# Pairwise bilinear products: x tiles and output slots in one SBUF tile, slots of 43 to 127 pairs

## The chip, the cores and the metric

The kernel runs on one core of a Trainium2 chip. The metric is the device time of one execution in microseconds (us); four runs of a kernel give its median. Beside them stands one profiled execution, whose trace records every instruction and every DMA packet. PE is the matrix engine, DVE the vector engine, SP the engine that here only issues DMAs.

## What is computed

For each of 4096 samples there are 32 fields of 64 numbers. Every field is multiplied by one 64 x 64 matrix, and for each of the 496 pairs of fields i < j the untransformed field i is multiplied, number by number, with the transformed field j:

```python
r_x:       (4096, 32, 64) float32
L0_rec_W:  (64, 64) float32

vid = jnp.einsum('bfd,de->bfe', x, W)
idx_i, idx_j = jnp.triu_indices(32, k=1)
return x[:, idx_i, :] * vid[:, idx_j, :]        # (4096, 496, 64)
```

Input is 33.6 MB, output 520.1 MB.

## The kernel before

The batch is cut into 16 tiles of 256 samples. In a tile, the 128 SBUF partitions are 2 halves of 64 features, and along a partition lie 32 fields of 128 samples (C = 128); a field of a partition is thus 512 bytes, an x tile 16 KiB of each partition, 2 MB in all. The host lays x out that way, pads each row of x in DRAM by 8 fields and each row of the output by 24, and puts the output back in order afterwards.

For a tile t, PE multiplies x by W into `vid`, which takes all of PSUM (L127: 8 groups of 4 fields, 2 halves each). DVE then multiplies pairs: one `tensor_tensor` (L151) takes a run of pairs, with x from SBUF and `vid` from PSUM as operands, and writes 128 x (pairs x 128) numbers to an output slot in SBUF. The order of the pairs is that of `by_block`, a recursive order in which runs are long; `products` cuts the runs where a slot ends, so the slot's size decides how many multiplies there are: 384 here.

Pairs are numbered through all 16 tiles, 0 to 7935, and slots know nothing of tiles. A slot has 84 pairs, 43,008 bytes of a partition (L135 to L155). Three slots are used in turn (`opool`, bufs=3). When a slot is full, SP stores it to its columns of the output with one DMA of 128 rows: 94 stores of 84 pairs, and one of 40 at the end.

x has 6 places (`xpool`). At the start SP loads tile 0 in four pieces and tiles 1 to 5 whole (L113). After the products of tile 4 it loads tiles 6 to 10, and after those of tile 9 tiles 11 to 15.

SP issues in the order in which the program is written. A DMA that must wait, for DVE to fill a slot or for a place of x to be used up, holds back all that is written after it. DVE, too, runs in program order; it writes to a slot only once the slot's earlier store has landed. The framework derives these waits from the places that each instruction reads and writes. Completions are counted on eight semaphores used in turn, so a DMA also waits for the one eight before it.

Of the kernel before, what the change touches and what calls it, by code (L numbers as in the profile page):

```python
# [1 line left out]

# [4 lines left out]

F32 = mybir.dt.float32
ALU = mybir.AluOpType

P = 128

C = 128

SLOT = 84

PLACES = 6

XPAD = 8
OPAD = 24  # L20


def by_block():


    def within(lo):
        yield "step", lo, 2, 1, 0
        for k in range(2):
            yield "step", lo, 4, 2, k
        for i in (lo, lo + 8):  # L30
            yield "row", i + 4, i, 4, 4
        yield "row", lo + 8, lo, 8, 8

    yield from within(0)
    yield "row", 16, 0, 16, 16
    yield from within(16)


def products(blocks, at=0):

    for kind, a, b, c, d in blocks:
        if kind == "row":
            rows, n, i0, di, j0, dj = c, d, b, 0, a, 1
        else:
            rows, n, i0, di, j0, dj = 16 // b, c, a, b, a + c + d, b
        r = k = 0
        while r < rows:
            room = SLOT - at % SLOT
            if k or room < n:
                m, w = 1, min(n - k, room)  # L50
            else:
                m, w = min(rows - r, room // n), n
            yield at, m, w, i0 + r * di + k, di, j0 + r * dj, dj
            at += m * w
            if k + w == n:
                r, k = r + m, 0
            else:
                k += w


def pairs(blocks):

    for _, m, w, i, di, j, dj in products(blocks):
        for r in range(m):
            for k in range(w):
                yield i + r * di + k, j + r * dj


@with_exitstack
def pairwise_bilinear_kernel(  # L70
    ctx: ExitStack,
    tc: tile.TileContext,
    x: bass.AP,
    w: bass.AP,
    out: bass.AP,
):

    nc = tc.nc
    NT = x.shape[0]
    F = x.shape[2] - XPAD
    D = P // 2
    NP = F * (F - 1) // 2

    BANK = 512 // C


    ctx.enter_context(tc.manual_schedule(engines={mybir.EngineType.SP}))  # L90

    const = ctx.enter_context(tc.tile_pool(name="const", bufs=1))
    xpool = ctx.enter_context(tc.tile_pool(name="x", bufs=PLACES))
    opool = ctx.enter_context(tc.tile_pool(name="out", bufs=3))
    psum = ctx.enter_context(
        tc.tile_pool(name="ps", bufs=1, space=bass.MemoryType.PSUM)
    )
    vid = psum.tile([P, F, C], F32)


    w2 = const.tile([P, D], F32)
    nc.sync.dma_start(out=w2, in_=w)  # L102

    loaded = []

    def load(pieces=1):
        t = len(loaded)
        if t == NT:
            return
        xt = xpool.tile([P, F, C], F32, tag="x", name=f"x_{t}")  # L110
        n = F // pieces
        for lo in range(0, F, n):
            nc.sync.dma_start(out=xt[:, lo : lo + n, :], in_=x[t][:, lo : lo + n, :])  # L113
        loaded.append(xt)

    load(4)
    for _ in range(PLACES - 1):
        load()

    for t in range(NT):  # L120
        xt = loaded[t]


        for b in range(0, F, BANK):
            for h in range(2):
                half = slice(h * D, (h + 1) * D)
                nc.tensor.matmul(  # L127
                    vid[half, b : b + BANK, :],
                    lhsT=w2[half, :],
                    rhs=xt[half, b : b + BANK, :],  # L130
                    start=True,
                    stop=True,
                )

        for at, m, w, i, di, j, dj in products(by_block(), t * NP):  # L135
            base = at - at % SLOT
            if at == base:
                ot = opool.tile([P, SLOT, C], F32, tag="o", name=f"o_{at}")
            n = m * w
            o = ot[:, at - base : at - base + n, :]  # L140
            if m == 1:
                left = xt[:, i : i + w, :]
                right = vid[:, j : j + 1, :].to_broadcast([P, w, C])
            else:
                o = o.rearrange("p (m w) c -> p m w c", m=m)
                right = vid[:, j : j + (m - 1) * dj + 1 : dj, :].unsqueeze(2).to_broadcast([P, m, w, C])
                if di == 0:
                    left = xt[:, i : i + w, :].unsqueeze(1).to_broadcast([P, m, w, C])
                else:
                    left = xt.rearrange("p (m d) c -> p m d c", d=di)[:, i // di : i // di + m, i % di : i % di + w, :]  # L150
            nc.vector.tensor_tensor(o, left, right, ALU.mult)  # L151
            at += n
            if at in (base + SLOT, NT * NP):
                nc.sync.dma_start(
                    out=out[:, base:at, :], in_=ot[:, : at - base, :]  # L155
                )


        if (t + 1) % (PLACES - 1) == 0:
            for _ in range(PLACES - 1):  # L160
                load()


_INS = ["r_x", "L0_rec_W"]
_OUTS = [((4096, 496, 64), "float32")]


# [37 lines left out]
```

## Time and profile before

| | us |
|---|---|
| median of 4 runs | 1290.59 (1290.42 to 1290.79) |
| the profiled execution | 1290.72 |
| its span, first to last instruction | 1288.9 |
| DVE busy, 384 multiplies | 1091.3 |
| PE busy, 512 matmuls | 224.2 |
| DVE waiting for stores to land | 160.1 |

The profile's page lists the DMAs by the line that issues them, with their size and the median time from issue to landing:

```profile
out_dram<-o SPq DMA_DIRECT2D x94, 5376.0 KB, 26.5
x<-in_r_x_dram SPq DMA_DIRECT2D x15, 2048.0 KB, 35.0
out_dram<-o SPq DMA_DIRECT2D x1, 2560.0 KB, 25.8
x<-in_r_x_dram SPq DMA_DIRECT2D x4, 512.0 KB, 5.4
```

A store is issued when DVE has filled its slot, and then lies in the queue behind the store before it; so the 26.5 us to landing hold about two transfers of 5.4 MB.

The page shows the bytes that the DMA engines moved, in 40 equal slices of the span:

```profile
GB/s 384 434 446 430 427 441 432 428 438 434 431 431 415 436 430 433 438 430 432 438 432 430 439 430 432 412 438 431 431 439 431 431 439 432 428 438 434 428 436 366
```

The first slice holds the start of the first loads, the 13th and the 26th (415 and 412) the two later groups of loads, the last one the end of the last store.

### The profile page before, as it was taken

The page shows a single profiled execution, that of the slowest core. Times are in us where ns is not written, and L with a number is a line of the kernel's source. Part 1 is how long each engine was busy: PE and PEld are TensorE (multiplying, and loading weights), DVE is VectorE, ACT ScalarE, POOL GpSimd, SP SyncE. Part 2 cuts the span into 40 slices and gives each one's busy share as a digit, 9 for nine tenths or more (in the row PEclk, how much of TensorE's full clock was granted, in tenths as well). Part 3 has the DMA queues.
Part 4 walks back from the last instruction along what each step waited for, and adds up shares of the span by engine and source line. Part 5 has one row for each costly group of instructions (what it writes and reads, how often), then busy time and mean ns, then how long its engine had stood idle before and what let it go on. Part 6 is the DMA issues. An engine that isn't in the chain of part 4 may idle for free.

```text
span 1288.9 us, 1785 instructions
## 1 busy us (share of the span) xinstructions
PE 224.2 (17%) x512; PEld 40.3 (3%) x512; DVE 1091.3 (85%) x384; POOL 0.2 (0%) x4
## 2 busy tenths in 40 slices
PE   4031211303122012030311301103021130312000
PEld 1000000000000000000000000000000000000000
DVE  6998888989897288898989989468989898988881
POOL 0000000000000000000000000000000000000000
PEclk7565565556556555555555655656555555655555
DMA  9999999999999999999999999999999999999998
GB/s 384 434 446 430 427 441 432 428 438 434 431 431 415 436 430 433 438 430 432 438 432 430 439 430 432 412 438 431 431 439 431 431 439 432 428 438 434 428 436 366
DMA packets 16570, 553.80 MB, mean 430 GB/s; under 512 B 1968, under 2 KB 1968, under 8 KB 2480
## 3 DMA queue, kind: packets, MB, share of 16 engines
q1 hardware_dynamic: 16560, 553.69, 99.7%
q8 instruction: 4, 0.07, 0.0%
q14 instruction: 6, 0.05, 0.0%
HBM read 33.59 MB, written 520.09 MB: 430 GB/s over the span
## 4 chain that ended last, share of the span: by engine, by line
DMA 60%; DVE 33%; another core or an unknown queue 5%; issue 0%; PE 0%; DVEq 0%; SPq 0%
DMA out_dram<-o 60%; DVE o L151 33%; PE vid L127 0%; DMA x<-in_r_x_dram 0%; DVEq L151 0%; SPq L102 0%
## 5 line engine op out<-in xcount | busy, mean ns | idle before, releaser
L151 DVE TENSOR_TENSOR o<-x,vid 128x1024 f32<-128x1024 f32 (+9 forms) x384 | 1091.3, 2905 | 170.8 <-DMA out_dram<-o 160.1
L127 PE MATMUL vid<-x,w 64*64 64x512 f32 x512 | 224.2, 995 | 966.3 <-DVE o L151 911.0
L127 PEld LDWEIGHTS vid<-x,w 64*64 64x64 f32 x512 | 40.3, 195 | 1148.6 <-DVE o L151 1060.6
L175 POOL MEMSET const-bfloat16-1.0<- 128x1 bf16 x1 | 0.1, 101 | 0.0
L175 POOL MEMSET const-uint8-127<- 128x1 uint8 x1 | 0.1, 101 | 0.0
L175 POOL MEMSET const-float32-0.0<- 128x1 f32 x1 | 0.1, 98 | 0.2 <-issue 0.2
L175 POOL MEMSET const-float32-1.0<- 128x1 f32 x1 | 0.1, 98 | 0.0
## 6 DMA issues: line engine op xcount, KB each, us to landing
out_dram<-o SPq DMA_DIRECT2D x94, 5376.0 KB, 26.5
x<-in_r_x_dram SPq DMA_DIRECT2D x15, 2048.0 KB, 35.0
out_dram<-o SPq DMA_DIRECT2D x1, 2560.0 KB, 25.8
x<-in_r_x_dram SPq DMA_DIRECT2D x4, 512.0 KB, 5.4
w<-in_L_rec_W_dram SPq DMA_DIRECT2D x1, 32.0 KB, 1.8
```

The lines of the kernel that those rows point to most:

```text
L127: nc.tensor.matmul(vid[half, b : b + BANK, :], lhsT=w2[half, :], rhs=xt[half, b : b + BANK, :], start=True, stop=True,)
L151: nc.vector.tensor_tensor(o, left, right, ALU.mult)
L175: nc = _bacc.Bacc("TRN2", target_bir_lowering=False, num_devices=1, dynamic_dma_scratch_size=1024)
```

## The change

x places and output slots are cut from one SBUF tile, `mem`, of 445 fields (pairs) of each partition, 227,840 bytes; before, the two pools had 6 x 32 + 3 x 84 = 444. `XPLACE` gives the place of each x tile in it, and `SLOTS` a list of 80 slots by size (43 to 127 pairs) and place. `STARTS` has the number of the first pair of each slot. Slots may lie where x tiles have been used up: tiles 0 to 4 and 6 to 10 take places 285 to 444, tile 5 takes 0 to 31, and tiles 11 to 15 take 128, 96, 64, 32 and 0. 58 of the 80 slots have more than 84 pairs, 8 have 84, and 14 fewer.

The loads keep their number, their sizes and their groups (6, 5 and 5 tiles, after the products of tiles 4 and 9). The order of the pairs is unchanged; runs are cut at other places, into 407 multiplies. In the changed file the matmul is at L150, the multiply at L174, the store at L177 and the load at L135.

```diff
-SLOT = 84
-
-PLACES = 6
+UNITS = 445
+
+GROUPS = [6, 5, 5]
+XPLACE = [285, 317, 349, 381, 413, 0, 285, 317, 349, 381, 413, 128, 96, 64, 32, 0]
+SLOTS = [
+    (127, 32), (126, 159), (63, 32), (64, 95), (84, 159), (63, 32),
...
+    (127, 243), (116, 127), (95, 32), (127, 243), (116, 127), (43, 370),
+    (95, 32), (95, 127), (63, 222), (95, 32), (84, 127), (74, 211),
...
+    (105, 0), (106, 105), (56, 211), (95, 267), (51, 362), (107, 160),
...
+    (116, 223), (106, 339), (127, 64), (127, 191), (127, 318), (127, 32),
+    (127, 159), (120, 286),
+]
+STARTS = [0, *accumulate(n for n, _ in SLOTS)]
...
-            room = SLOT - at % SLOT
+            room = STARTS[bisect_right(STARTS, at)] - at
...
-    xpool = ctx.enter_context(tc.tile_pool(name="x", bufs=PLACES))
-    opool = ctx.enter_context(tc.tile_pool(name="out", bufs=3))
+    mem = const.tile([P, UNITS, C], F32)
...
-        xt = xpool.tile([P, F, C], F32, tag="x", name=f"x_{t}")
+        xt = mem[:, XPLACE[t] : XPLACE[t] + F, :]
...
-            base = at - at % SLOT
-            if at == base:
-                ot = opool.tile([P, SLOT, C], F32, tag="o", name=f"o_{at}")
+            slot = bisect_right(STARTS, at) - 1
             n = m * w
-            o = ot[:, at - base : at - base + n, :]
+            begin, end = STARTS[slot], STARTS[slot + 1]
+            ot = mem[:, SLOTS[slot][1] : SLOTS[slot][1] + SLOTS[slot][0], :]
+            o = ot[:, at - begin : at - begin + n, :]
...
-            if at in (base + SLOT, NT * NP):
-                nc.sync.dma_start(
-                    out=out[:, base:at, :], in_=ot[:, : at - base, :]
-                )
+            if at == end:
+                nc.sync.dma_start(out=out[:, begin:end, :], in_=ot)
-        if (t + 1) % (PLACES - 1) == 0:
-            for _ in range(PLACES - 1):
+        if t + 2 == len(loaded) < NT:
+            for _ in range(next(groups)):
                 load()
```

In the prediction, slots, stores and x tiles are numbered from 0.

## The prediction

> **What bounds the kernel now.** I read the page's DMA rows first, since the kernel writes 520 MB, then the chain of waits, the waits of each engine, and the multiplies by shape; last, the trace's DMA packet records, grouped by size. The page:
>
> ```profile
> span 1288.9 us, 1785 instructions
> PE 224.2 (17%) x512; PEld 40.3 (3%) x512; DVE 1091.3 (85%) x384; POOL 0.2 (0%) x4
> DMA  9999999999999999999999999999999999999998
> q1 hardware_dynamic: 16560, 553.69, 99.7%
> HBM read 33.59 MB, written 520.09 MB: 430 GB/s over the span
> ```
>
> The one queue that SP fills keeps the 16 DMA engines occupied for 99.7% of the span; VectorE (DVE) has 15% to spare. The chain of waits, in a steady stretch (start us, length us, what):
>
> ```profile
> 1000.31 26.54 DMA out_dram<-o
> 1026.94 11.56 DVE o L151 x4
> 1038.52 26.50 DMA out_dram<-o
> 1065.11 11.49 DVE o L151 x3
> 1076.62 26.56 DMA out_dram<-o
> 1103.28 11.62 DVE o L151 x5
> 1114.92 26.51 DMA out_dram<-o
> ```
>
> The chain alternates because a slot is written again as soon as its store has landed. From 1000.31 to 1114.92 are nine stores of 84 pairs: 114.61 / 9 = 12.73 us each. A DVE slot takes 11.5 us, so DVE waits for the DMA, never the reverse, as the waits of DVE say:
>
> ```profile
> DVE o L151 <- DMA out_dram<-o: 160.1, 92, 27.1
> ```
>
> (us in total, times, longest.) So only the sum of what the DMA engines must do, and any hole in their work, can move the end.
>
> The packet records price that work. A DMA of 128 rows is 128 packets, 8 to each engine, and a 4-byte completion on each. Commonest durations: 4,096 bytes 159 ns, 16,384 611, 20,480 761, 43,008 1,589, loads and stores alike; a completion 9 ns. The line through the last two is (1589 - 761) / (43008 - 20480) = 0.03675 ns per byte and 8.3 ns for the packet itself; it gives 159 and 611 for the other two sizes. A pair is 512 bytes of a row, so a store of n pairs takes 8 x (8.3 + 18.82 n) + 9 ns = 0.075 + 0.1505 n us: 12.72 for 84, as in the chain. Packets lie end to end from 10 us to 1280 us.
>
> What the packets took above that line adds up to 4.5 us per engine on average: 1.1 at the first loads and the first stores after them, 1.5 around the loads of 390 to 430 us, 1.3 at those of 800 to 830, the rest scattered. The engines do not share it equally: the first is done at 1283.5 us, the average one at 1284.7, the last at 1287.45.
>
> **The change, part by part.**
>
> *Fewer, longer stores.* 95 stores become 80 with the same 7,936 pairs. No bytes go. 15 x 128 packets go, 120 per engine at 8.3 ns: 1.00 us. 15 completions at 9 ns: 0.13 us. Sum: -1.13 us, on the path that sets the end. 58 of the stores have rows longer than 43,008 bytes (up to 127 x 512 = 65,024), which no row here shows. Bounds per such packet: below, its bytes at the rate seen with no fixed part (-8.3 ns); above, the line once more broken in two, +8.3 ns. 58 x 8 = 464 such packets per engine make this -3.9 to +3.9 us. I take 0, as four sizes lie on one line.
>
> The Trainium skill's "DMA: Bandwidth & Descriptors" (Anatomy of one DMA) puts a fixed cost of about 2.0 us on each DMA, of the path that GpSimd issues. By that rule 15 stores fewer would be an estimated 30 us, a time near 1260; the chain's 12.73 us for bytes that take 12.65 at the packet rate leaves 0.08 us per store, so I go by the row.
>
> *Multiplies.* Other slot edges cut the same products into 407 multiplies in place of 384.
>
> ```profile
> L151 DVE TENSOR_TENSOR o<-x,vid 128x8192 f32<-128x8192 f32 x32 | 277.8, 8681 | 1.9 <-DMA out_dram<-o 1.9
> L151 DVE TENSOR_TENSOR o<-x,vid 128x1024 f32<-128x1024 f32 x129 | 151.8, 1216 | 62.3 <-DMA out_dram<-o 51.6 <-PE vid L127 10.6
> ```
>
> (8681 - 1216) / 7168 is 1.041 ns an element, 133.3 ns a pair. 84-pair slots in the chain take 11.43 us with 2 multiplies and 11.75 with 7: 0.064 us for each more. 23 more: 1.5 us of DVE, under the 160.1 us in which it waits for stores. Without that cover it would cost those 1.5 us. 83 more groups of multiplies in the built stream wait on DVE's own earlier ones, since x and slots now share a tile; at most the 0.15 us fixed part of a 1216 ns multiply each, 12 us in all, again inside the 160.
>
> *First store later.* Slot 0 has 127 pairs in 7 multiplies. DVE starts at 10.63 us; 127 x 0.1336 + 7 x 0.064 = 17.4, so the store is issued near 28.1 us and not 22.4. From issue to first packet took 1.0 us at the start (0.73 to 1.73). The loads occupy the engines until 32.6 to 33.7 us, so 29.1 is in time by 3.5 us. Cost 0; if the loads were done sooner, each us would count.
>
> *Slots that wait for others.* Store 0 then ends near 33.0 + 19.2 = 52.2. Slot 1 (126 pairs) is ready at 45.2: in time by 6. Slots 2 and 3 lie where slot 0 was; they start once it has landed (0.45 us after the last packet, as at the end of the trace, and 0.7 for the late engines): 53.4 + 8.6 + 8.8 = 70.8. Slot 4 needs store 1 landed, 71.2 + 1.2 = 72.4, and is ready at 84.0, its first packet 85.0; stores 2 and 3 occupy the DMA until 71.2 + 9.6 + 9.7 = 90.5. In time by 5.5 us. I carried these two columns (ready, and DMA free) on through all 80 stores. After slot 4 the least is 7 us, at store 10 and at the load of x_11; in the later part DVE is up to 20 us ahead.
>
> *Loads.* x_6 to x_10 are issued after store 24, and the last of their places is freed by store 23; store 24 and two loads, 14.4 + 2 x 4.9 = 24 us, lie in the queue meanwhile. x_11 waits for store 49, whose place it takes; SP, which issues in order, stands still, and behind x_11 wait four loads and store 51, whose products are ready. Store 50 alone, 56 pairs, 8.5 us, covers the landing and the issue, 0.45 + 1.0. In time by 7 us; uncovered it would cost 1.5 us. The loads' own bytes and packets are unchanged.
>
> *End.* The last store grows from 40 to 120 pairs, but its slot is ready some 20 us before the DMA gets to it, where before it was 14. The spread between engines stays as it is. Cost 0.
>
> Sum: the profiled execution took 1290.72 us, 1.8 of it around the span; less 1.13 is 1289.6. That run lies 0.13 over the median 1290.59, so the median becomes 1289.5.
>
> **Rivals.**
>
> *Faster than the sum (1287.3).* The 4.5 us above the line and the 2.75 us by which the last engine trails the average belong to no byte. If the extras around the two later load groups fell more evenly, the last engine could gain up to that 2.75. The floor is 1284.5: the changed packets by the line alone, 1279.3 us per engine, 1.9 before the first of them, 1.5 from the last to the end of the span, 1.8 around it. For it: these extras lie where loads meet stores, and the stores beside them change. Against it: there are still three groups of loads, of the same tiles. With half of the two groups' 2.8 us gone and 0.8 of the spread, 2.2 in all: 1289.5 - 2.2 = 1287.3.
>
> *Slower: long rows cost more than the line (1293.4).* Place: packets over 43,008 bytes, at every one of the 58 longer stores. Break-even is 1.13 us / 464 = 2.4 ns a packet. At one more fixed part each, 8.3 ns, it is +3.9: 1289.5 + 3.9 = 1293.4, just over the bound for slower. For it: nothing so long is in the trace. Against it: no bend from 4,096 to 43,008.
>
> *Slower: a hole at x_11 or store 4.* Decides when landing plus issue takes over 8.5 us (now 1.5). To lose the 3.8 us that reach 1293.3 it would have to be 12.3. In the chain DVE starts 0.1 us after a landing (1000.31 + 26.54 = 1026.85; it starts at 1026.94), which speaks against it.
>
> *It doesn't do what it says.* If one tile made every multiply wait for every store, DVE and DMA would take turns, 1091 + 1280 = 2370 us. The built streams' waits name single stores.
>
> **How the numbers follow.** No change is what lies within 0.2%, 2.6 us, about what a measurement of this kernel can tell: 1288.0 to 1293.2. Forecast 0.64 (own range 1288.4 to 1290.7: 0.4 of spread from run to run and 0.8 for extras that fall on other engines), faster 0.20, long rows 0.12, a hole 0.03, false waits 0.01. So faster 0.20, within 0.64, slower 0.16. The range 1287.0 to 1292.2 leaves out the long-row case at its full price, the hole, the false waits and the best quarter of the faster case, 0.2 in all; it takes in some 6 of the 8.3 ns of the long-row bound.
>
> **What would show it.** 14,400 packets on the queue in place of 16,560 (15 x 144 fewer, completions among them); 99.7% occupied again; packets of 65,024 bytes at 2,398 ns (another figure there falls the size term); no slice under 400 GB/s but the first and the last; store 0 issued near 28 us; SP standing before x_11 with DMA full. A DMA slice with a hole, or GB/s that falls where rows are longest, would make the prediction wrong; so would a last engine that trails by more than 2.75 us.

## The result, and the profile after

The changed kernel takes 1289.29 us (median of 41 runs, 1288.93 to 1290.16), the kernel before 1290.61 (61 runs, 1290.19 to 1291.36). The ratio is 0.999, its 95% interval 0.9986 to 0.9995: 1.3 us faster, between 0.6 and 1.8. The forecast was 1289.5. The profiled execution took 1289.63 us, 1.09 less than that of before.

The page of the changed kernel, the rows that answer to those of before:

```profile
span 1287.9 us, 1768 instructions
PE 221.9 (17%) x512; PEld 41.0 (3%) x512; DVE 1087.9 (84%) x407; POOL 0.2 (0%) x4
DMA  9999999999999999999999999999999999999998
GB/s 387 451 416 443 426 430 448 433 435 431 424 435 412 433 435 431 439 428 438 429 444 437 422 438 421 426 431 436 430 437 435 432 433 437 435 433 433 430 442 359
q1 hardware_dynamic: 14400, 553.69, 99.7%
HBM read 33.59 MB, written 520.09 MB: 430 GB/s over the span
```

The bytes are the same and the occupied share is the same, 99.7%; only the packets are fewer, 14,400 for 16,560, as counted in the prediction. No slice but the first and the last is under 412 GB/s, and by the packet records an engine stood idle for some 0.1 us on average between 10 us and the end of the first engine (before: 0.2): the DMA never ran dry.

The packet records of the new sizes, beside what the line drawn through the sizes of before gives (8.3 ns and 0.03675 ns a byte):

| bytes of a packet | by the line, ns | commonest in the trace of the changed kernel, ns |
|---|---|---|
| 22,016 | 817 | 818 |
| 48,640 | 1796 | 1796 |
| 59,392 | 2191 | 2192 |
| 65,024 | 2398 | 2399 |

The first multiplies and gaps of DVE (start us, length us, what, and in brackets the idle time before it and what ended it):

```profile
10.86 34.47 DVE L174 TENSOR_TENSOR mem<-mem,vid 128x1024 f32<-128x1024 f32 x10 [10.86 <-PE vid L150]
53.20 17.41 DVE L174 TENSOR_TENSOR mem<-mem,vid 128x1408 f32<-128x1408 f32 x6 [7.87 <-DMA out_dram<-mem]
72.20 30.66 DVE L174 TENSOR_TENSOR mem<-mem,vid 128x512 f32<-128x512 f32 x17 [1.58 <-issue]
```

Slots 0 and 1 are filled without a break, from 10.86 to 45.3; then DVE stands for 7.87 us until store 0 has landed (the prediction had 53.4 for the 53.20 here, and 72.4 for the 72.20). The DMAs that SP issued:

```profile
28.36 334.62 SPq L177 DMA_DIRECT2D out_dram<-mem  x25
363.16 25.05 SPq L135 DMA_DIRECT2D mem<-in_r_x_dram  x5
392.03 382.87 SPq L177 DMA_DIRECT2D out_dram<-mem  x26
798.75 5.68 SPq L135 DMA_DIRECT2D mem<-in_r_x_dram  x5
804.47 439.43 SPq L177 DMA_DIRECT2D out_dram<-mem  x29
```

The first store goes out at 28.36 (28.1 foretold). Before the loads at 798.75 SP stood still for store 49, the longer of two such waits of SP's queue (us in total, times, longest):

```profile
SPq L135 <- DMA out_dram<-mem: 43.4, 2, 23.8
```

These 23.8 us cost nothing: by the packet records store 50 occupied the engines from 795.4 to 806.7, and the first packet of x_11 began at 804.4, on the engine that was done first. The other wait, 19.6 us, lies inside the load group issued from 363.16 on. And DVE waits less often, but not much less in all, with fewer and longer slots (before: 160.1 us in 92 waits):

```profile
DVE mem L174 <- DMA out_dram<-mem: 143.1, 34, 27.3
```

### The profile page after: what moved, and what is told of

It is laid out like the page before. It is cut to its first block, busy times and chain, and to the rows that moved or that the text cites. A ratio compares the mean times of both kernels' runs of the same rounds, so it can differ in the third digit from the quotient of the medians.

```text
span 1287.9 us, 1768 instructions
## 1 busy us (share of the span) xinstructions
PE 221.9 (17%) x512; PEld 41.0 (3%) x512; DVE 1087.9 (84%) x407; POOL 0.2 (0%) x4
## 3 DMA queue, kind: packets, MB, share of 16 engines
q1 hardware_dynamic: 14400, 553.69, 99.7%
## 4 chain that ended last, share of the span: by engine, by line
DMA 48%; DVE 45%; issue 3%; SPq 0%; PE 0%; another core or an unknown queue 0%; DVEq 0%
DMA out_dram<-mem 47%; DVE mem L174 45%; SPq L135 0%; PE vid L150 0%; DMA mem<-in_r_x_dram 0%; DVEq L214 0%; DVEq L174 0%; SPq L126 0%
## 5 line engine op out<-in xcount | busy, mean ns | idle before, releaser
L174 DVE TENSOR_TENSOR mem<-mem,vid 128x1024 f32<-128x1024 f32 (+16 forms) x407 | 1087.9, 2748 | 155.7 <-DMA out_dram<-mem 143.1
L150 PE MATMUL vid<-mem,w 64*64 64x512 f32 x512 | 221.9, 990 | 953.7 <-DVE mem L174 901.2
L150 PEld LDWEIGHTS vid<-mem,w 64*64 64x64 f32 x512 | 41.0, 196 | 1132.9 <-DVE mem L174 1044.4
```

What stands on the lines that cost most here:

```text
L150: nc.tensor.matmul(vid[half, b : b + BANK, :], lhsT=w2[half, :], rhs=xt[half, b : b + BANK, :], start=True, stop=True,)
```

## The experiments

"Theory" in the expectations is that of the prediction. Each time stands beside runs of the kernel before on the same chip.

### e1: twice the stores

```diff
-                nc.sync.dma_start(
-                    out=out[:, base:at, :], in_=ot[:, : at - base, :]
-                )
+                half = (at - base) // 2
+                for lo in (0, half):
+                    nc.sync.dma_start(
+                        out=out[:, base + lo : base + lo + half, :], in_=ot[:, lo : lo + half, :]
+                    )
```

> The kernel before, with each of its 95 stores issued as two DMAs of half the slot, from the same slot and after the same multiply: 95 stores more, 128 packets and 16 completions each, the same bytes. Theory (8.3 ns a packet, 9 ns a completion, per DMA engine, on the path): 95 x 0.075 = +7.1 us, 1297.7. Rival (a large fixed cost of a DMA, about 2 us each): +190 us, 1480. Rival (packets and completions are hidden, the gain of the change came from elsewhere): 0, 1290.6.

Measured: 1298.32 us beside 1290.78, ratio 1.0058 (1.0045 to 1.0072). That is 7.54 us for 95 more stores, 79 ns each (61 to 98); 75 were expected. A microsecond or two per store is ruled out, and so is nothing. Of the 79 ns, 9 are the completion by its own record, so some 8.8 ns fall on each of the eight packets of an engine.

### e2: twice the packets, the same stores

```diff
+                half = (at - base) // 2
+                place = base + 2 * (base // SLOT)
+                to = out[:, place : place + 2 * (half + 1), :].rearrange("p (h n) c -> p h n c", h=2)
                 nc.sync.dma_start(
-                    out=out[:, base:at, :], in_=ot[:, : at - base, :]
+                    out=to[:, :, :half, :],
+                    in_=ot[:, : at - base, :].rearrange("p (h n) c -> p h n c", h=2),
                 )
...
-    laid = (2 * D, NT * shape[1] + OPAD, C)
+    laid = (2 * D, NT * shape[1] + 488, C)
...
```

(What is left out picks the two parts of each row out of the wider output again, on the host.)

> The kernel before, with each store still one DMA, but its rows in two parts that lie apart in the output: 128 packets more for each of 95 stores, no completion more. Theory: 95 x 8 x 8.3 ns = +6.3 us, 1296.9, and packets of 21,504 bytes take 799 ns. If what costs is the DMA or its completion and not the packet: 0 to +0.9 us, 1290.6 to 1291.5.

Measured: 1299.20 us beside 1290.78, ratio 1.0066 (1.0050 to 1.0081): +8.4 us, 11 ns a packet (8.5 to 13.8). So it is the packet that costs, not the DMA nor its completion. The size is over the 8.3 ns of the line, though its interval meets that of e1. The commonest packet of 21,504 bytes takes the expected 799 ns, but the mean is 803.7, where 43,008 bytes had a mean only 2 ns over their commonest. Rows of the output also lie at another pitch here; but in e1, where the pitch is that of before, packets of this size have a mean of 802.7 too, so the pitch does not explain the longer mean.

### e3: the shared tile alone

```diff
-XPLACE = [285, 317, 349, 381, 413, 0, 285, 317, 349, 381, 413, 128, 96, 64, 32, 0]
+XPLACE = [32 * (t % 6) for t in range(16)]
-SLOTS = [
...
-]
+SLOTS = [(min(84, 7936 - at), 192 + 84 * (at // 84 % 3)) for at in range(0, 7936, 84)]
```

(against the changed kernel)

> The changed kernel with slots of 84 pairs at three places and x at six places of the one tile, as before: 95 stores. Theory (only the number of packets counts): 1290.6. Rival (the shared tile itself changes waits or the speed of DVE or DMA): for the whole of the gain to come from it, 1289.3; if it costs something that the longer slots gave back, over 1291.

Measured: 1290.91 us beside 1290.78, ratio 1.0002 (0.9993 to 1.0011). By the interval the tile shared by x and slots is worth 0.9 us at the most and costs 1.4 at the most; the change's 1.3 us do not come from it alone, the gain needs the longer slots.

### e4: the longest slots without the list

```diff
-SLOT = 84
+SLOT = 126
...
-    opool = ctx.enter_context(tc.tile_pool(name="out", bufs=3))
+    opool = ctx.enter_context(tc.tile_pool(name="out", bufs=2))
```

> The kernel before with two slots of 126 pairs in place of three of 84: 63 stores. Packets: 32 stores fewer, 32 x 0.075 = -2.4 us, 1288.2, if the DMA stays fed. A store takes 19.04 us; in that time one slot must be seen to have landed, be filled (126 x 0.1336 + some 5 x 0.064 = 17.2 us) and its store's first packet start: 1.9 us for landing and issue. Theory with 0.45 + 1.0 = 1.45 us for these: 1288.2, DMA at 99.7%. If they take 2.2 us in truth (late engines, or a slower issue), 62 x 0.3 is lost, 1307 at most, and the DMA shows holes at every store: then what bounds the length of the slots is the latency, and the list of the changed kernel is what hides it.

Measured: 1298.61 us beside 1290.78, ratio 1.0061 (1.0047 to 1.0074): 63 stores, and 7.8 us slower. The page of e4:

```profile
GB/s 386 449 414 446 424 404 446 414 446 424 436 446 396 437 446 412 416 444 416 440 420 446 414 446 405 426 416 446 414 446 444 416 414 446 444 416 414 446 414 410
q1 hardware_dynamic: 11952, 553.69, 99.2%
```

The chain of waits of e4 (start us, length us, what):

```profile
502.97 17.16 DVE o L151 x4
520.13 0.02 issue
520.14 20.73 DMA out_dram<-o
540.87 0.03 issue
540.90 0.02 DVEq L151
540.92 0.04 issue
540.97 17.42 DVE o L151 x8
558.38 0.02 issue
558.40 20.47 DMA out_dram<-o
```

A store that is issued at 520.14 lands 20.73 us later, 1.7 more than its own 19.04 us of transfer: it found the queue all but empty. One round of two stores, 520.14 to 558.40, takes 38.26 us where two transfers take 38.08. The packet records show the DMA idle for 10.2 us of the execution, 3.8 before; and the packets of 64,512 bytes take 2,390 ns on average, 2,380 where the changed kernel has such packets. The 32 stores saved are more than lost. So a longer slot pays only while another store covers the landing, the filling and the issue; two equal slots leave no such cover, the list of mixed sizes does.

### e5: loads one at a time

```diff
-        if (t + 1) % (PLACES - 1) == 0:
-            for _ in range(PLACES - 1):
-                load()
+        if len(loaded) < NT:
+            load()
```

> The kernel before, with tiles 6 to 15 loaded one at a time, each after the products of a tile, in place of two groups of five: the same loads, stores, packets and bytes, ten places where loads stand among stores in place of two. The packets around the two groups took some 1.4 us each above the line. Theory A (that belongs to each change between stores and loads): 8 places more, +8 x 1.4 = +11 us, 1302. Theory B (it belongs to the loaded bytes): 0, 1290.6. Theory C (it is spread thinner, as single loads disturb less, the faster case of the prediction): down to 1288.

Measured: 1297.43 us beside 1290.85, ratio 1.0048 (1.0035 to 1.0061): +6.6, and Theory C falls: single loads are not gentler. The page of e5:

```profile
DMA  9999999999999999999999999999999999999996
GB/s 384 436 431 433 440 428 426 431 440 426 434 437 425 434 435 424 435 435 424 437 424 430 438 431 428 428 436 430 434 433 435 435 434 434 429 434 433 433 437 279
```

The last slice is the one to see: 279 GB/s, where it was 366. Most engines are done and wait for two. By the packet records the average engine ends at 1285.8 us, 1.1 later than before. But 12 of the 16 end as before; the last two end at 1293.9 and 1294.9, some 7.4 us later than the last two of before, and the two ahead of them 1.2 and 2.0 later. Eight more places where loads stand among stores thus cost the last engine 0.9 us each, and most others nothing. Of the three theories A fits, but it put the 1.4 us of the average engine where the 0.9 of the last one belongs. Why two engines bear nearly all of it stays open.

### e6 and e7: half and twice the matmuls

e6 puts W twice on the diagonal of a zeroed 128 x 128 tile; e7 halves the columns of a matmul. Both are edits of the kernel before.

```diff
e6
-    w2 = const.tile([P, D], F32)
-    nc.sync.dma_start(out=w2, in_=w)
+    w2 = const.tile([P, P], F32)
+    nc.vector.memset(w2, 0.0)
...
     load(4)
+    for h in range(2):
+        nc.sync.dma_start(out=w2[h * D : (h + 1) * D, h * D : (h + 1) * D], in_=w[h * D : (h + 1) * D, :])
...
-                    vid[half, b : b + BANK, :],
-                    lhsT=w2[half, :],
-                    rhs=xt[half, b : b + BANK, :],
+                vid[:, b : b + BANK, :],
+                lhsT=w2,
+                rhs=xt[:, b : b + BANK, :],
e7
-        for b in range(0, F, BANK):
+        for b in range(0, F, BANK // 2):
...
-                    vid[half, b : b + BANK, :],
+                    vid[half, b : b + BANK // 2, :],
...
-                    rhs=xt[half, b : b + BANK, :],
+                    rhs=xt[half, b : b + BANK // 2, :],
```

> The kernel before, with W twice on the diagonal of one 128 x 128 weight tile and one matmul for both halves: 256 matmuls and weight loads in place of 512. PE is not on the path. The trace has four packets of 16,384 bytes and some six of 8,192 in the span that are no loads of the kernel and lie on the instruction queues. Theory D (these are fetched instructions of PE, on the DMA engines, and make the last engine trail the average by 2.75 us): about half of the four go, some 2 x 0.6 = 1.2 us for the last engine if it carries them, 1289.4; no less than 0.3 if they are spread. Rival (they are something else or on engines that end early): 1290.6, and the last engine trails as before.

> The kernel before, with matmuls of 256 columns, 1024 of them in place of 512 with as many weight loads more. Theory D: 1024 instructions more are some four packets of 16,384 bytes more on the instruction queue, +0.6 us each on the engines that carry them: 1291.2 to 1293.0. Rival: 1290.6.

Measured beside 1290.85: e6 1289.69, ratio 0.999 (0.9982 to 0.9999); e7 1292.54, ratio 1.0013 (1.0004 to 1.0022). The instruction queue on the page of before, of e6 and of e7 (packets, MB, share):

```profile
q8 instruction: 4, 0.07, 0.0%
```

```profile
q8 instruction: 2, 0.03, 0.0%
```

```profile
q8 instruction: 8, 0.13, 0.0%
```

The packets of 16,384 bytes go as the matmuls do, 4, 2 and 8, and so does the time, -1.2 us (-2.3 to -0.1) and +1.7 (0.5 to 2.8), though PE is idle four fifths of the time in all three. The last engine ended at 1287.45, 1286.22 and 1289.17.

The packet records name no engine, but the packets of an engine follow one another within a few ns and can be chained. At 163.33 us of the kernel before, a packet of 16,384 bytes on the instruction queue begins where a store packet ends; it takes 960 ns, the store packet behind it 1,967 in place of 1,589, and the engine is 1.3 us late from then on. So it is, by 1.28 to 1.33 us, at all eleven such packets of the three runs that lie clear of the loads: twice the 0.6 that Theory D reckoned with. That fetched instructions share the DMA engines with the stores is shown by this. That the end moves because the last engine carries them is not shown: behind the last loads, the fetch of the kernel before, at 1101 us, lies on an engine that ends at 1284.86, 2.6 us ahead of the last, while that of e6, at 969 us, lies on the last engine itself.

### e8 and e9: the changed kernel with half the matmuls

e8 is the edit of e6 on the changed kernel, with 768 bytes of scratch for DMA descriptors (1,024 before) to make room; e9 moves W ahead.

```diff
e9 against e8
     load(4)
-    for h in range(2):
-        nc.sync.dma_start(out=w2[h * D : (h + 1) * D, h * D : (h + 1) * D], in_=w[h * D : (h + 1) * D, :])
...
             nc.sync.dma_start(out=xt[:, lo : lo + n, :], in_=x[t][:, lo : lo + n, :])
+            if t == 0 and lo == n:
+                for h in range(2):
+                    nc.sync.dma_start(out=w2[h * D : (h + 1) * D, h * D : (h + 1) * D], in_=w[h * D : (h + 1) * D, :])
```

> The changed kernel with the single weight tile and half the matmuls (scratch for DMA descriptors of 768 in place of 1,024 bytes, to make room for the larger weight tile). If theory D holds and adds to the change: 1289.3 - 1.2 = 1288.1, faster than both kernels. If not: 1289.3.

Measured: 1291.07 beside 1290.85, ratio 1.0 (0.9991 to 1.0009): the change's gain is gone. Stretches of the changed kernel, and of e8 (time, then PE, PEld, DVE and POOL busy, clock, DMA share and GB/s):

```profile
30.00:32.00 2.00, 1.07 (x4) 0.00 (x0) 2.00 (x1) 0.00 (x0) 0.50 1.02 377
32.00:34.00 2.00, 0.00 (x0) 0.00 (x0) 2.00 (x1) 0.00 (x0) 0.50 1.55 651
```

```profile
30.00:32.00 2.00, 0.00 (x0) 0.00 (x0) 2.00 (x1) 0.00 (x0) 0.50 0.96 410
32.00:34.00 2.00, 1.72 (x2) 0.84 (x3) 2.00 (x3) 0.00 (x0) 0.50 0.06 25
```

A packet's bytes are counted where it begins, so 651 is the start of store 0. In e8 nothing begins: W lies in the queue behind tile 0, the first multiply starts at 15.76 instead of 10.86, and store 0 is issued at 33.26, when the loads have run out. This is the hole that the prediction priced at 0 with 3.5 us to spare and at one for one beyond: 4.9 us of delay less 3.5 is 1.4, and the DMA stood idle for 1.8, as the loads ended sooner too (at 32.1 to 32.7 us, in the changed kernel at 32.8 to 33.6).

> The kernel of e8 with W issued between the second and the third piece of tile 0, not behind the fourth. In e8 the first multiply began at 15.76 us and not at 10.86, the first store was issued at 33.26 and not at 28.36, when the loads had run out, and from 32 to 34 us the DMA engines moved 25 GB/s in place of 651. Theory (a hole of 1.8 us there hid what half the matmuls gained): the first multiply before 13 us, no slice with a hole, 1289.3 - 1.2 = 1288.1 to 1291.07 - 1.8 = 1289.3. Rival (half the matmuls or the smaller scratch do not go with long slots): 1291.0 again, without a hole.

Measured: 1288.90 beside 1290.97, ratio 0.9983 (0.9974 to 0.9992). The first multiply is at 12.46 and the hole is gone, with 610 GB/s from 32 to 34 us: a cause shown by taking it away. What was 0.2 us over the kernel before is now 2.1 under it; of these 2.3 us the hole accounts for 1.8, and the rest lies inside the intervals.

### e10 and e11: the changed kernel and e9 side by side

> The changed kernel once more, beside e11 on one chip: 1289.3 if the kernel before gives 1290.6, a ratio of 0.999.

> The kernel of e9 once more, beside e10 on one chip. If half the matmuls are worth what e6 showed on the kernel before (-1.2 us): 1.2 us under e10. If the gain of e9 was the chip's: within 0.3 us of e10.

Measured beside 1290.95: the changed kernel 1289.37, ratio 0.9988 (0.9979 to 0.9997); the kernel of e9 1288.85, ratio 0.9984 (0.9975 to 0.9993). It is 0.5 us under the changed kernel, between what the two theories expected (1.2, and at most 0.3), and the intervals overlap: it beats the kernel before, but not surely the changed one. Whether half the matmuls are worth less here than the 1.2 us of e6 stays open; the interval of e6 takes in 0.5.

## Why the prediction was right, point by point

*The bound.* Right. The DMA engines are occupied for the same share, and e3 shows that the shared tile by itself does not make the gain. The prediction did not see that instructions fetched for PE are work of the DMA engines too (e6 and e7); but before and after have four such packets each.

*Fewer, longer stores: -1.13 us.* Right in kind and size: -1.09 between the profiled executions, -1.3 between the medians (0.6 to 1.8). The price per store was tested by e1 (75 ns foretold, 79 measured) and put on the packet by e2, where it came out at 11 ns rather than 8.3; at these two prices the 15 stores are worth 1.2 to 1.5 us. That the profiled executions come within 0.04 us of the sum is in part luck: one fetch of instructions makes its engine 1.3 us late, and in e10 the changed kernel lies 1.6 us under the kernel before. What does not hang on the last engine agrees: the average engine ends at 1283.75 us in place of 1284.70, and what packets take above the line is 4.7 us per engine, 4.6 before.

The 2 us that the Trainium skill's "DMA: Bandwidth & Descriptors" (Anatomy of one DMA) gives as the fixed cost of one DMA, on the path that GpSimd issues, are seen neither in the change nor in e1, where one more store in a full queue cost 79 ns. Where the queue has all but run out, in e4, the two stores shown land 1.4 and 1.7 us beyond their transfer.

*Long rows.* The rival with 8.3 ns more for each packet over 43,008 bytes is refuted by the records: 2,399 ns for 65,024 bytes, one more than the line gives.

*Multiplies: 23 more, 1.5 us of DVE, hidden.* Hidden, yes; but the busy time of DVE fell by 3.4 us. The sum of their durations, 1115.4 us before, is 1118.5 after (407 x 2748 ns), so the multiplies did take longer in sum. But busy time counts overlaps once, and multiplies that follow on one another overlap, by 0.08 us each in both traces (24.2 us over 291 successions, 30.6 over 371); across a wait they do not, and there are 34 waits for stores in place of 92. No wait of DVE on its own earlier multiplies shows among its waits.

*The first store, and the slots that wait.* Right within 0.3 us at four places: 28.36 for 28.1, 53.20 for 53.4, 72.20 for 72.4, store 4 issued at 83.90 for 84.0. That the margin is real was shown by e8, which used it up.

*The load of x_11.* SP stood for 23.8 us without cost. The 7 us to spare were some 5: issued at 798.75 with 1.0 to its first packet, it could have begun at 799.75, and the first engine was free at 804.4. The prediction left out how far the engines lie apart: store 49 has landed only when its last engine is done, at 798.23, and the first engine had gone on to store 50 at 795.42, 2.8 us sooner.

*The end.* The last engine trails the average by 2.6 us in place of 2.75. The prediction left this spread as it was, and was right to; its faster rival, in which it shrinks because loads disturb less, did not happen, and in e5 it grows when loads stand among stores at eight places more. Its own price for that case came from the average engine, and the last one sets the end.

## What to carry to other kernels

Where one queue keeps the DMA engines occupied for the whole span, count packets and bytes, draw a line through the packet durations of a few sizes, and look for holes; what other engines do enters through holes, and through the instructions that are fetched for them. Longer stores save some 8 to 11 ns for each packet that goes and take away cover: for each wait, set the time that a landing, a filling and an issue take against the transfers still queued, as e4 and e8 show on both sides of that edge. The last DMA engine ends the kernel, not the average one, so look at how far apart they end.

## What the runs showed of the hardware that was not expected

Instructions of a mostly idle engine cost DMA time: 512 instructions fewer or 1024 more on PE, which was busy 17% of the span in the kernel before, moved the end by -1.2 and +1.7 us, with packets of 16,384 bytes on an instruction queue, 4 in the span before, 2 and 8 in these. Each makes the DMA engine that carries it 1.3 us late.

Loads among stores delay mainly two of the 16 DMA engines: 0.9 us for each place on the last two, 0.14 on the average (1.1 us for eight), nothing on twelve.
